# A self-attention block and a residual block on one core: the softmax exponential in two parts, and weight halves kept between image stages that follow each other

## The chip, the core and the metric

The kernel runs on one core of a Trainium2 chip. Its engines work side by side, each on its own stream of instructions: TensorE (PE) multiplies matrices, VectorE (DVE) does elementwise work on two operands, ScalarE (ACT) applies functions to one operand, and GpSimd (POOL) and SyncE (SP) here mostly start transfers. Data lies in DRAM, in the on-chip SBUF (128 partitions), and in PSUM, where TensorE's products are summed. An instruction waits until what it reads has been written and until the buffer it writes is free. An engine's instructions, and a queue's transfer starts, are issued in the order of the program, so one that waits holds those behind it.

The metric is the time of one execution in microseconds (us): 2428.24 us, the median of 3 runs (2428.1 to 2429.0).

## What is computed

Two bottleneck blocks, one after the other, over 16 images of 1024 channels and 32 x 32 pixels, in float32. The first has a local self-attention in its middle, the second a 3x3 convolution. Cut to what matters:

```python
# layer 0: 1x1 to 256 channels, attention over the 3x3 neighbourhood, 1x1 back, residual
h = relu(bn(conv1x1(x, w_conv1)))
q = relu(bn(conv1x1(h, wq)));  k = relu(bn(conv1x1(h, wk)));  v = bn(conv1x1(h, wv))
attn = einsum('bgdhw,bgdkhw->bgkhw', q_heads, unfold3x3(k) + pos)   # 32 heads of 8 channels, 9 taps
attn = softmax(attn, over the 9 taps)
h = relu(bn(einsum('bgdkhw,bgkhw->bgdhw', unfold3x3(v), attn)))
x = relu(bn(conv1x1(h, w_conv3)) + x)
# layer 1: 1x1 to 256 channels, 3x3, 1x1 back, residual
y = relu(bn(conv1x1(x, w1)))
y = relu(bn(conv3x3(y, w2)))
return relu(bn(conv1x1(y, w3)) + x)
```

## The kernel before

The order of TensorE's work is a fixed list of stages. `C` is the first convolution of an image, `Q` its q, k and position products, `V` its v (`P` stands for all three), `F` the fused stage (w_conv3, residual, and the second block's first convolution at once), `W` the 3x3 convolution of four images by the Winograd method, `U` the last convolution of an image. `U10:0123` is a part of the output channels.

```python
"P0 P1 P2 P3 F0 P4 F1 P5 P6 F2 P7 F3 C8 Q8 W0 V8 C9 U0 Q9 V9 U1 U2 U3",
"F4 F5 F6 F7 P10 C11 Q11 W4 V11 C12 U4 Q12 V12 U5 U6 U7",
"F8 F9 P13 F10 F11 C14 Q14 W8 V14 C15 U8 Q15 V15 U9",
"F12 F13 F14 U10:0123 F15 U10:4567 U11:01234 W12 U11:567 U12 U13 U14 U15",
```

VectorE's work is laid beside it by a small model that runs while the program is written: a class `Side` keeps an estimated time of TensorE and one of VectorE and decides after each step of TensorE which pieces of attention or of the Winograd transform are placed next. The values that a piece yields are its estimated us; `EXP` is the time allowed for the exponential, `LATE` how long a transform stands behind attention.

```python
CHUNK, RELAY, EXP, LATE = 3.43, 13.0, 3.0, 30.0
```

The attention of one image is all VectorE but for the exponential, which ScalarE does. `e` holds the 9 taps (256 pixels per partition and tap):

```python
def logits(b):
    ...                                   # 9 taps: products q*k, sums over 8 channels, positions
    mx = apool.tile([P, JPIX], F32, tag="mx", name="mx")
    tree(ALU.max, mx)
    yield 2.7
    nc.vector.tensor_tensor(e, e, mx.unsqueeze(1).to_broadcast([P, KK, JPIX]), ALU.subtract)
    yield 2.6

    yield lambda: nc.scalar.activation(e, e, AF.Exp)
    make_room("qk", b + 1)
    se = apool.tile([P, JPIX], F32, tag="mx", name="se")
    tree(ALU.add, se)
    nc.vector.reciprocal(se, se)
    yield 3.9
    weights_of[b] = e, se

def weighted(b):
    ...
    if b == B - 1:
        fetch_hidden(DEFERRED[0])
    term(0, acc)                          # e[0] * v at tap 0
    yield 2.3
    for k in range(1, KK):
        term(k, t)
        nc.vector.tensor_add(acc, acc, t)
        yield 4.6
    nc.vector.tensor_mul(acc, acc, se ...)
    nc.sync.dma_start(back, acc ...)      # "a" by way of DRAM, read again by the fused stage
    make_room("v", b + 1)
```

q, k and the positions are stored to DRAM from a layout by channels and read again in one by heads and rows; the reading is `relay`, all three tiles at once when the image before has made room:

```python
def relay(what, b):
    if not ((what, b) in written and (what, b) in room_for):
        return
    come[what, b] = max(side.vector, side.tensor) if b else side.tensor
    ...
    for name, tag, shape in shapes:       # q, bnk, pos; or bnv
        t = apool.tile([P] + shape, F32, tag=tag, name=f"{tag}_{b}")
        nc.gpsimd.dma_start(t.rearrange("p d w -> p (d w)"), backs[name])
        moved[name] = ...
```

k and v go out of one buffer, `kp`, by SyncE's queue, the same one that loads the weights and stores the transformed images (`v<-v`):

```python
norm(inside(kp, n), rows(conv(which, n)), name, n, func)    # ScalarE writes kp
nc.sync.dma_start(room[n], AP(block.tensor, ...))           # "bnk<-kp", "bnv<-kp"
```

Weights come in halves of 512 KB into five buffers, four in flight or in use; a new one is loaded when one has had its last use. A fused stage takes four halves, always loaded anew:

```python
if kind == "fused":
    return [("w3", 0), ("u1", 0), ("w3", 1), ("u1", 1)]
...
        before, whose = near.get((name, half), (-9, b))
        if at - before > 3 or name in ("w3", "u1"):
            whose = (b, at)
            queue.append((name, whose, half))
```

In the fused stage the second block's hidden rows end in one buffer, `vh`, from which the Winograd transform of the image is made. Two of the images of the last group store them to DRAM instead, and their transforms are made while F15 runs:

```python
DEFERRED = 13, 14

def fused(b, then):
    side.finish(b)                        # what is left of the image's attention
    if b == B - 1:
        for c in DEFERRED:
            side.first(transform(c, sources[c]) if c in sources else fetched(c), 0.0, 0.0)
    fetch_attended()
    ...
    for o in range(NC + 1):
        if o < NC:
            conv3.products(o)
            ...
        if o:
            reduce_part(o - 1, ps, done.pop(o - 1), "u1")
            if o == NC:
                ...                       # hidden rows into vh
                if b in DEFERRED:
                    kept[b] = dram.tile([P, NW * VROWS * VW], F32, tag=f"h{b}", name="kept")
                    nc.sync.dma_start(kept[b], vh.rearrange("p r w -> p (r w)"))
                else:
                    late = 0.0 if b % NK == NK - 1 else LATE
                    side.first(transform(b, vh), side.tensor + CHUNK + 6.0, side.tensor + late)
```

Of the kernel before, what the change touches and what calls it, by code (L numbers as in the profile page):

```python
# [8 lines left out]
F32 = mybir.dt.float32  # L9
# [4 lines left out]
P = 128  # L14
# [7 lines left out]
KK = 9  # L22
# [7 lines left out]
PW = W + 2  # L30
HALO = (JROWS + 2) * PW
NPOS = 4
G = P // HEAD_DIM
NH = NW * G

# [36 lines left out]
def sa_bottleneck_kernel(ctx: ExitStack, tc: tile.TileContext, x, w1t, wqkvt, w3t, u1t, u2t, u3t, params, out):  # L72
# [275 lines left out]
    def piece(name, half):  # L348
        return name, owner[now[0], name, half], half

    def reduce_part(c, ps, src, name):

        key = piece(name, c * 2 // NC)
        wt = pieces[key]
        for n in range(NW):
            for half in range(2):
                nc.tensor.matmul(  # L357
                    ps[n][:, halves(half)],
                    wt[:, c % (NC // 2), n * P : (n + 1) * P],
                    src[:, halves(half)],  # L360
                    start=(c == 0),
                    stop=(c == NC - 1),
                )
        if c % (NC // 2) == NC // 2 - 1:
            done_with(key)
# [65 lines left out]
    hidden, projected, attended = {}, {}, {}  # L431


    CHUNK, RELAY, EXP, LATE = 3.43, 13.0, 3.0, 30.0

    def by_quarter(name, b, width, per):

# [84 lines left out]

    relaid, written, room_for, come = {}, set(), {("qk", 0), ("v", 0)}, {}

    def relay(what, b):

        if not ((what, b) in written and (what, b) in room_for):
            return  # L530
        come[what, b] = max(side.vector, side.tensor) if b else side.tensor
        moved, backs = projected.setdefault(b, {}), relaid[b]
        if what == "qk":
            shapes = (("q", "qc", [HEAD_DIM, JPIX]), ("bnk", "bnk", [HEAD_DIM, HALO]), ("pos", "pc", [NPOS, JPIX]))
        else:
            shapes = (("bnv", "bnv", [HEAD_DIM, HALO]),)
        for name, tag, shape in shapes:
            t = apool.tile([P] + shape, F32, tag=tag, name=f"{tag}_{b}")
            nc.gpsimd.dma_start(t.rearrange("p d w -> p (d w)"), backs[name])
            moved[name] = t.rearrange("p d (r w) -> p d r w", w=PW) if shape[1] == HALO else t  # L540

    def make_room(what, b):
        room_for.add((what, b))
# [5 lines left out]
    def logits(b):  # L549

        qc, kc = (projected[b][name] for name in ("q", "bnk"))
        e = apool.tile([P, KK, JPIX], F32, tag="e", name=f"e_{b}")
        t = ppool.tile([P, 2, HEAD_DIM, JPIX], F32, tag="t", name="prod")
        for k in range(0, KK, 2):
            of = min(2, KK - k)
            for two in range(of):
                i, j = divmod(k + two, 3)
                nc.vector.tensor_tensor(  # L558
                    by_row(t[:, two]), by_row(qc), kc[:, :, i : i + JROWS, j : j + W], ALU.mult
                )  # L560
# [12 lines left out]
        part = by_tap[:, :, 0:2]  # L573
        nc.vector.tensor_tensor(part, part, pc[:, 2:4].unsqueeze(1).to_broadcast(shape), ALU.add)
        yield 3.5

        def tree(op, to):
            t = zpool.tile([P, 4, JPIX], F32, tag="z", name="tree")
            nc.vector.tensor_tensor(t, e[:, 0:4, :], e[:, 4:8, :], op)
            nc.vector.tensor_tensor(t[:, 0:2, :], t[:, 0:2, :], t[:, 2:4, :], op)  # L580
            nc.vector.tensor_tensor(to, t[:, 0, :], t[:, 1, :], op)
            nc.vector.tensor_tensor(to, to, e[:, 8, :], op)

        mx = apool.tile([P, JPIX], F32, tag="mx", name="mx")
        tree(ALU.max, mx)
        yield 2.7
        nc.vector.tensor_tensor(e, e, mx.unsqueeze(1).to_broadcast([P, KK, JPIX]), ALU.subtract)
        yield 2.6

        yield lambda: nc.scalar.activation(e, e, AF.Exp)  # L590
        make_room("qk", b + 1)
        se = apool.tile([P, JPIX], F32, tag="mx", name="se")
        tree(ALU.add, se)
        nc.vector.reciprocal(se, se)
        yield 3.9
        weights_of[b] = e, se

    weights_of = {}

    def weighted(b):  # L600

        e, se = weights_of.pop(b)
        vc = projected.pop(b)["bnv"]
        both = ppool.tile([P, 2, HEAD_DIM, JPIX], F32, tag="t", name="acc")
        acc, t = both[:, 0], both[:, 1]

        def term(k, dst):
            i, j = divmod(k, 3)
            nc.vector.tensor_tensor(  # L609
                by_row(dst),  # L610
                rows(e[:, k, :]).unsqueeze(1).to_broadcast([P, HEAD_DIM, JROWS, W]),
                vc[:, :, i : i + JROWS, j : j + W],
                ALU.mult,
            )

        if b == B - 1:
            fetch_hidden(DEFERRED[0])
        term(0, acc)
        yield 2.3
        for k in range(1, KK):  # L620
            term(k, t)
            nc.vector.tensor_add(acc, acc, t)  # L622
            yield 4.6
        nc.vector.tensor_mul(acc, acc, se.unsqueeze(1).to_broadcast([P, HEAD_DIM, JPIX]))
        summed[b], back = by_quarter("a", b, JPIX, HEAD_DIM)
        nc.sync.dma_start(back, acc.rearrange("p d w -> p (d w)"))
        make_room("v", b + 1)
        side.ready[b] = side.vector + 2.3 + RELAY
        fetch_attended()
        yield 2.3  # L630
# [210 lines left out]
    class Side:  # L841
# [32 lines left out]
        def step(self):  # L874
            job, self.vector = self.begins()
            if self.exp and not self.held and ("needs" in job or self.exp[0] < self.tensor):
                self.fire()
            cost = next(job["parts"], "end")
            if cost == "end":
                (self.jobs if "needs" in job else self.firsts).remove(job)  # L880
            elif "needs" not in job:
                job["begun"] = True
                cost, rest = cost if isinstance(cost, tuple) else (cost, 0.0)
                self.vector += cost
                job["at"] = self.vector + rest
            elif cost == "v":
                job["needs"] = cost
            elif callable(cost):
                self.exp = self.vector, cost
                if job["b"] == 0:  # L890

                    self.held = True
            else:
                self.vector += cost
# [22 lines left out]
        def passes(self, us, leave=True):  # L917

            self.tensor += us
            if leave:  # L920
                self.run()

# [2 lines left out]
            self.vector = max(self.vector, self.tensor) + us  # L925

        def finish(self, b):
            while any(job["b"] == b for job in self.jobs):
                if self.exp and not self.firsts:
                    self.tensor = max(self.tensor, self.exp[0])  # L930
# [15 lines left out]
    for text in (  # L946
# [5 lines left out]
        for word in text.split():  # L952
            b, _, of = word[1:].partition(":")
            for letter in "CQV" if word[0] == "P" else word[0]:
                kind = {"C": "conv1", "Q": "qk", "V": "v", "F": "fused", "W": "wino", "U": "u3"}[letter]
                stages.append((kind, int(b), [int(o) for o in of] or range(NC)))

    def weights_of_stage(kind, b, of):
        if kind == "conv1":
# [3 lines left out]
        if kind == "v":  # L963
            return [("wv", 0)]
        if kind == "fused":
            return [("w3", 0), ("u1", 0), ("w3", 1), ("u1", 1)]
        if kind == "wino":
            return [(f"U{i}", part) for two in ROWS for part in range(3) for i in two]
        if kind == "u3":
# [5 lines left out]
    for at, (kind, b, of) in enumerate(stages):  # L975
        for name, half in weights_of_stage(kind, b, of):
            before, whose = near.get((name, half), (-9, b))
            if at - before > 3 or name in ("w3", "u1"):
                whose = (b, at)
                queue.append((name, whose, half))  # L980
            owner[at, name, half] = whose
# [31 lines left out]
        return AP(vh.tensor, vh.offset + (n * VROWS + 1) * VW, [vh.ap[0], [9, 4], [VW, H], [1, TR]])  # L1013


    DEFERRED = 13, 14
    kept = {}

    sources = {}
# [9 lines left out]
        yield 0.0, 6.0  # L1029
        yield from transform(b, sources[b])  # L1030

    def fused(b, then):

        side.finish(b)
        if b == B - 1:
# [4 lines left out]
        finish_attended(b)  # L1040
        conv3 = expand("w3", b)
        conv3.src = attended.pop(b)
        following = [(conv3, o) for o in range(2, NC)] + then
        done, ps = {}, None
        for o in range(NC + 1):
            if o < NC:
                conv3.products(o)
                room = stored[b, o] = dram.tile([P, HW], F32, tag=f"r{b}_{o}", name="r")
                done[o] = conv3.result(o, room)
                if o < len(following):  # L1050
                    into, which = following[o]
                    into.seed(which)
                yield CHUNK
            if o:
                ps = ps or two_sums()
                reduce_part(o - 1, ps, done.pop(o - 1), "u1")
                if o == NC:
# [37 lines left out]
    def run(at):  # L1095
# [6 lines left out]
                break  # L1102
        fetch_attended()
        if kind == "fused":
            parts, count = fused(b, then), 2 * NC
        elif kind == "u3":
            parts, count = last_sum(b, of, then), len(of)
        elif kind == "conv1":
# [93 lines left out]
```

## Time and profile before

| | busy, us | share of the span |
|---|---|---|
| TensorE, matmuls | 2387.5 | 98% |
| VectorE | 2081.2 | 86% |
| ScalarE | 917.0 | 38% |
| GpSimd | 467.8 | 19% |
| moved by transfers | 708.38 MB | mean 292 GB/s |

The span of the profiled execution, from its first to its last instruction, is 2426.4 us. A line of the waits says which engine and tile waited, `<-` for whom, how long in total, how many times and the longest. A line of a timeline gives start, duration, engine, line of the program, operation, `out<-in` by the program's names, the shape, the count merged into it, and in brackets the idle time ahead of it with what ended it. `SPq` and `POOL` lines with `DMA` are the starts of transfers, not the transfers. A line of the stretches has, behind the busy time and the count of each engine, three columns: the clock that TensorE was granted (1.00 is full), the share of the transfer engines, and GB/s.

### The profile page before, as it was taken

Reading aid. Unit: us, or ns where it says so; the run is one execution under the profiler, and the core shown is the slowest. Engines: PE = TensorE matmul, PEld = TensorE weight load, DVE = VectorE, ACT = ScalarE, POOL = GpSimd, SP = SyncE. Lnnn points to the kernel's source line nnn. Section 1 sums busy time; section 2 is a strip of 40 time slices with the busy share of each in tenths; the row PEclk is TensorE's granted clock in tenths of the full one; section 3 lists DMA queues with packets and bytes.
Section 4 is the critical chain, followed back from the end, with each engine's and each line's share of the span. In section 5 each row is a group of like instructions: output and inputs, shape, how many; then the busy total and the mean of one; then the engine's idle time right before and its main releaser. Section 6 shows DMA issues by size and latency. Waiting matters only on the chain.

```text
span 2426.4 us, 18497 instructions
## 1 busy us (share of the span) xinstructions
PE 2387.5 (98%) x6144; PEld 1150.3 (47%) x6144; DVE 2081.2 (86%) x1632; ACT 917.0 (38%) x873; POOL 467.8 (19%) x854
## 2 busy tenths in 40 slices
PE   8999999999999999999999999999999999999999
PEld 3443434444466444444466444444466444434844
DVE  4899988999999989999989999998989999965700
ACT  3323242233222474433122574324222553344265
POOL 2111111111111232111111232112111221112132
PEclk9999999999999999999999999999999999999999
DMA  9969686887797899797788998689788897888887
GB/s 359 360 208 313 228 274 227 258 300 236 288 310 254 333 355 352 261 307 250 246 296 277 318 375 337 238 287 320 244 307 305 310 350 250 279 310 292 320 295 251
DMA packets 305822, 708.38 MB, mean 292 GB/s; under 512 B 20544, under 2 KB 174144, under 8 KB 297024
## 3 DMA queue, kind: packets, MB, share of 16 engines
q0 software_dynamic: 119024, 471.40, 53.3%
q1 hardware_dynamic: 185264, 231.30, 29.7%
q10 hardware_dynamic: 1440, 4.51, 0.5%
q8 instruction: 49, 0.80, 0.1%
q14 instruction: 45, 0.37, 0.0%
HBM read 432.10 MB, written 275.03 MB: 291 GB/s over the span
## 4 chain that ended last, share of the span: by engine, by line
PE 85%; DMA 5%; DVE 5%; issue 2%; ACT 1%; POOL 1%; SPq 0%; ACTq 0%; POOLq 0%; DVEq 0%
PE ps L357 34%; PE ps L389 30%; PE ps L452 11%; PE ps L744 8%; DMA U<-uw 2%; DVE acc L609 2%; DVE acc L622 2%; DMA bnk<-kp 1%; PE ps L490 1%; DMA a<-acc 1%; DMA a<-a 1%; ACT h L1004 1%; DMA uw<-u 0%; POOL out_dram L417 0%; DMA v<-v 0%
## 5 line engine op out<-in xcount | busy, mean ns | idle before, releaser
L389 PE MATMUL ps<-a,w 128*128 128x512 f32 x1024 | 461.7, 596 | 5.1 <-ACT a L648 4.8
L357 PE MATMUL ps<-result,u 128*128 128x512 f32 x1024 | 460.1, 594 | 6.6 <-ACT result L416 6.6
L357 PE MATMUL ps<-x,w 128*128 128x512 f32 x1024 | 445.1, 595 | 6.2 <-DMA x<-in_x_dram 6.2
L389 PE MATMUL ps<-y,u 128*128 128x512 f32 x1024 | 443.2, 594 | 4.2 <-ACT ps L380 4.2
L609 DVE TENSOR_TENSOR acc<-e,bnv 128x2048 f32<-128x2048 f32 x144 | 327.6, 2284 | 3.6
L558 DVE TENSOR_TENSOR prod<-qc,bnk 128x2048 f32<-128x2048 f32 x144 | 324.1, 2287 | 1.7
L389 PEld LDWEIGHTS ps<-a,w 128*128 128x128 f32 x1024 | 195.2, 191 | 253.5 <-issue 243.0
L357 PEld LDWEIGHTS ps<-result,u 128*128 128x128 f32 x1024 | 194.9, 191 | 254.0 <-issue 238.1
L357 PEld LDWEIGHTS ps<-x,w 128*128 128x128 f32 x1024 | 195.6, 191 | 252.5 <-issue 252.0
L389 PEld LDWEIGHTS ps<-y,u 128*128 128x128 f32 x1024 | 194.9, 191 | 250.6 <-issue 241.0
L416 ACT ACTIVATE result<-ps,par 128x1024 f32<-128x1024 f32 x128 | 142.5, 1113 | 442.6 <-PE ps L389 371.6
L622 DVE TENSOR_TENSOR acc<-acc 128x2048 f32<-128x2048 f32 x128 | 293.4, 2292 | 4.4
L452 PE MATMUL ps<-h,wqk 128*128 128x512 f32 x512 | 225.8, 595 | 5.7 <-ACT h L1004 5.7
L417 POOL DMA_DIRECT2D r<-result x128 | 69.0, 539 | 637.3 <-ACT result L416 622.4
L416 ACT ACTIVATE result<-ps,bn_sh 128x1024 f32<-128x1024 f32 x127 | 141.2, 1112 | 133.0 <-PE ps L389 122.4
L563 DVE TENSOR_TENSOR prod<-prod 128x2048 f32<-128x2048 f32 (+1 forms) x80 | 166.2, 2077 | 2.4
L452 PEld LDWEIGHTS ps<-h,wqk 128*128 128x128 f32 x512 | 96.2, 190 | 132.7 <-issue 110.0
L1004 ACT ACTIVATE h<-ps,par 128x1024 f32<-128x1024 f32 x32 | 38.4, 1204 | 283.2 <-PE ps L357 283.0
L380 ACT ACTIVATE ps<-r 128x1024 f32<-128x1024 f32 x128 | 130.4, 1020 | 29.3 <-DMA r<-r 21.8
L464 ACT ACTIVATE kp<-ps,par 128x1024 f32<-128x1024 f32 x64 | 77.4, 1210 | 168.5 <-PE ps L452 125.7
L380 ACT ACTIVATE ps<-s 128x1024 f32<-128x1024 f32 x128 | 131.2, 1025 | 2.5
L339 POOL DMA_DIRECT2D x<-in_x_dram x120 | 64.0, 534 | 298.2 <-PE ps L357 231.2
(317 smaller groups left out, 2294.5 us busy)
## 6 DMA issues: line engine op xcount, KB each, us to landing
s<-in_x_dram POOLq DMA_DIRECT2D x128, 512.0 KB, 7.1
r<-result POOLq DMA_DIRECT2D x128, 512.0 KB, 4.8
r<-r POOLq DMA_DIRECT2D x128, 512.0 KB, 6.5
out_dram<-result POOLq DMA_DIRECT2D x127, 512.0 KB, 6.3
x<-in_x_dram POOLq DMA_DIRECT2D x120, 512.0 KB, 5.0
v<-v SPq DMA_DIRECT2D x96, 408.0 KB, 4.4
U<-uw SPq DMA_DIRECT2D x72, 512.0 KB, 5.5
bnk<-kp SPq DMA_DIRECT2D x32, 680.0 KB, 7.8
```

Source lines behind the costliest of these rows:

```text
L357: nc.tensor.matmul(ps[n][:, halves(half)], wt[:, c % (NC // 2), n * P : (n + 1) * P], src[:, halves(half)], start=(c == 0), stop=(c == NC ...
L380: nc.scalar.activation(ps, loaded.pop((self.kind, self.b, o)), AF.Identity)
L389: nc.tensor.matmul(self.ahead[o][:, halves(half)], pieces[key][:, n, o % (NC // 2) * P :][:, :P], self.src[:, n, halves(half)], start=Fals ...
L416: nc.scalar.activation(to_, ps, RELU, bias=self.shift(o), scale=1.0)
L417: nc.gpsimd.dma_start(to, t)
L452: nc.tensor.matmul(ps[:, halves(half)], pieces[key][:, m, at : at + P], h[:, m, halves(half)], start=(m == 0), stop=(m == NW - 1),)
L464: nc.scalar.activation(dst, src, func, bias=col(f"L0_conv_{name}_b", n), scale=col(f"L0_conv_{name}_s", n),)
L558: nc.vector.tensor_tensor(by_row(t[:, two]), by_row(qc), kc[:, :, i : i + JROWS, j : j + W], ALU.mult)
L563: nc.vector.tensor_add(u[:, :, 0:4], u[:, :, 0:4], u[:, :, 4:8])
L609: nc.vector.tensor_tensor(by_row(dst), rows(e[:, k, :]).unsqueeze(1).to_broadcast([P, HEAD_DIM, JROWS, W]), vc[:, :, i : i + JROWS, j : j ...
L622: nc.vector.tensor_add(acc, acc, t)
L744: nc.tensor.matmul(acc[i][:, at, :, n, :], pieces[key][:, m, at, n * P : (n + 1) * P], v[:, at, :, m * (TILES + TR) :][:, :, :TILES], star ...
```

## The change

It has four parts.

- The subtraction of the maximum and the exponential are made in two parts, of 4 and of 5 taps. The sum over the taps and its reciprocal move from ahead of the weighted terms to behind the first four of them, so that VectorE has terms of the first part to work on while ScalarE does the second. The model's figures follow (`EXP` 2.0).
- A fused stage that directly follows another one takes over the halves of the weights that lie there. Its output channels run in the reverse order of halves, so that it begins with those that the one ahead ended with.
- Of the last group only image 13's hidden rows are sent through DRAM; image 14's transform is made from `vh`, as for other images.
- From image 2 on, the three tiles of a relay are fetched one after the other, `GAP` (5 us of TensorE's model time) apart.

```diff
+FIRST = 4
...
-    def reduce_part(c, ps, src, name):
+    def reduce_part(c, ps, src, name, first=0, last=NC - 1):
...
-                    start=(c == 0),
-                    stop=(c == NC - 1),
+                    start=(c == first),
+                    stop=(c == last),
...
-    CHUNK, RELAY, EXP, LATE = 3.43, 13.0, 3.0, 30.0
+    GAP = 5.0
+    CHUNK, RELAY, EXP, LATE = 3.43, 13.0, 2.0, 30.0
...
+    moves = []
+    def more_moves(now):
+        while moves and moves[0][0] <= now:
+            moves.pop(0)[1]()
...
-        come[what, b] = max(side.vector, side.tensor) if b else side.tensor
...
-        for name, tag, shape in shapes:
+        def move(name, tag, shape):
             t = apool.tile([P] + shape, F32, tag=tag, name=f"{tag}_{b}")
             nc.gpsimd.dma_start(t.rearrange("p d w -> p (d w)"), backs[name])
             moved[name] = ...
+            if len(moved) in (3, 4):
+                come[what, b] = max(side.vector, side.tensor) if b else side.tensor
+        for i, shape in enumerate(shapes):
+            if b < 2 or i == 0:
+                move(*shape)
+            else:
+                moves.append((side.tensor + GAP * i, lambda shape=shape: move(*shape)))
...
-        nc.vector.tensor_tensor(e, e, mx.unsqueeze(1).to_broadcast([P, KK, JPIX]), ALU.subtract)
-        yield 2.6
-        yield lambda: nc.scalar.activation(e, e, AF.Exp)
+        parts = [e[:, :FIRST], e[:, FIRST:]]
+        for part in parts:
+            nc.vector.tensor_tensor(
+                part, part, mx.unsqueeze(1).to_broadcast([P, part.shape[1], JPIX]), ALU.subtract
+            )
+        yield 2.7
+        def exps():
+            for part in parts:
+                nc.scalar.activation(part, part, AF.Exp)
+        yield exps
         make_room("qk", b + 1)
-        se = apool.tile([P, JPIX], F32, tag="mx", name="se")
-        tree(ALU.add, se)
-        nc.vector.reciprocal(se, se)
-        yield 3.9
-        weights_of[b] = e, se
+        weights_of[b] = e, tree
...
-        if b == B - 1:
+        if b == B - 1 and DEFERRED and DEFERRED[0] in kept:
             fetch_hidden(DEFERRED[0])
         term(0, acc)
         yield 2.3
         for k in range(1, KK):
+            if k == FIRST:
+                se = apool.tile([P, JPIX], F32, tag="mx", name="se")
+                tree(ALU.add, se)
+                nc.vector.reciprocal(se, se)
+                yield 4.6
             term(k, t)
...
+                if kind == "fused" and stages and stages[-1][0] == "fused" and stages[-1][2][0] == 0:
+                    order = order[NC // 2 :] + order[: NC // 2]
...
-            return [("w3", 0), ("u1", 0), ("w3", 1), ("u1", 1)]
+            return [(name, half) for half in (of[0] * 2 // NC, of[-1] * 2 // NC) for name in ("w3", "u1")]
...
-            if at - before > 3 or name in ("w3", "u1"):
+            if at - before > (3 if name[1:] != "3" and name != "u1" or name == "u3" else 1):
...
-    DEFERRED = 13, 14
+    DEFERRED = (13,)
...
-    def fused(b, then):
+    def fused(b, of, then):
...
-        for o in range(NC + 1):
-            if o < NC:
+        for at in range(NC + 1):
+            if at < NC:
+                o = of[at]
```

More of the change, by code (lines that the diff above doesn't have):

```diff
@@ L586, in logits @@
         yield 2.7
-        nc.vector.tensor_tensor(e, e, mx.unsqueeze(1).to_broadcast([P, KK, JPIX]), ALU.subtract)
-        yield 2.6
-        yield lambda: nc.scalar.activation(e, e, AF.Exp)
-        make_room("qk", b + 1)
-        se = apool.tile([P, JPIX], F32, tag="mx", name="se")
-        tree(ALU.add, se)
-        nc.vector.reciprocal(se, se)
-        yield 3.9
-        weights_of[b] = e, se
+        parts = [e[:, :FIRST], e[:, FIRST:]]
[8 more added lines that the diff above has]
+        yield exps
+        make_room("qk", b + 1)
+        weights_of[b] = e, tree
     weights_of = {}
     def weighted(b):
-        e, se = weights_of.pop(b)
+        e, tree = weights_of.pop(b)
         vc = projected.pop(b)["bnv"]
@@ L888, in step @@
             elif callable(cost):
-                self.exp = self.vector, cost
+                self.exp = self.vector - 0.0, cost
                 if job["b"] == 0:
@@ L919, in passes @@
             self.tensor += us
+            more_moves(self.tensor)
             if leave:
@@ L927, in finish @@
         def finish(self, b):
+            more_moves(1e6)
             while any(job["b"] == b for job in self.jobs):
@@ L955, in sa_bottleneck_kernel @@
                 kind = {"C": "conv1", "Q": "qk", "V": "v", "F": "fused", "W": "wino", "U": "u3"}[letter]
-                stages.append((kind, int(b), [int(o) for o in of] or range(NC)))
+                order = [int(o) for o in of] or list(range(NC))
+                if kind == "fused" and stages and stages[-1][0] == "fused" and stages[-1][2][0] == 0:
+                    order = order[NC // 2 :] + order[: NC // 2]
+                stages.append((kind, int(b), order))
     def weights_of_stage(kind, b, of):
@@ L1042, in fused @@
         conv3.src = attended.pop(b)
-        following = [(conv3, o) for o in range(2, NC)] + then
+        following = [(conv3, o) for o in of[2:]] + then
         done, ps = {}, None
-        for o in range(NC + 1):
-            if o < NC:
+        for at in range(NC + 1):
+            if at < NC:
+                o = of[at]
                 conv3.products(o)
@@ L1049, in fused @@
                 done[o] = conv3.result(o, room)
-                if o < len(following):
-                    into, which = following[o]
+                if at < len(following):
+                    into, which = following[at]
                     into.seed(which)
                 yield CHUNK
-            if o:
+            if at:
                 ps = ps or two_sums()
-                reduce_part(o - 1, ps, done.pop(o - 1), "u1")
-                if o == NC:
+                reduce_part(of[at - 1], ps, done.pop(of[at - 1]), "u1", of[0], of[-1])
+                if at == NC:
                     side.finish_firsts()
@@ L1104, in run @@
         if kind == "fused":
-            parts, count = fused(b, then), 2 * NC
+            parts, count = fused(b, of, then), 2 * NC
         elif kind == "u3":
```

## The prediction

> **What bounds the kernel now.** I read the page's first part, then the waits of TensorE, then the timelines of the stretches where those waits fall.
>
> ```profile
> PE 2387.5 (98%) x6144; PEld 1150.3 (47%) x6144; DVE 2081.2 (86%) x1632; ACT 917.0 (38%) x873; POOL 467.8 (19%) x854
> ```
>
> TensorE is busy for 98% of the span, VectorE for 86%. So the order of matmuls is the bound and everything else matters only where TensorE waits. A busy share says little of the pitch, so I made a floor of it from the timeline: 8 matmuls of 512 columns start every 3.43 us, 0.429 us each; the 288 matmuls of an undisturbed 3x3 stage take 62.3 us, 0.216 us each; the 8 position products 1.87 us. That gives 4864 x 0.429 + 1152 x 0.216 + 128 x 0.233 = 2367 us. With 6.2 us ahead of the first matmul and 4.8 us after the last it makes 2378 us, of a span of 2426.4. **About 49 us can be lost to waits at all**, and nothing in the change removes a matmul.
>
> ```profile
> engine line waited for: us in total, times, longest us
> PE ps L357 <- ACT result L416: 6.6, 2, 5.2
> PE ps L357 <- DMA x<-in_x_dram: 6.2, 1, 6.2
> PE ps L452 <- ACT h L1004: 5.7, 13, 0.4
> PE ps L389 <- ACT a L648: 4.8, 2, 4.3
> PE ps L389 <- ACT ps L380: 4.5, 3, 3.2
> PE ps L744 <- DMA U<-uw: 4.2, 4, 1.7
> ```
>
> These are few and single waits. By stage, as the excess over the pitch: image 0's fused stage F0 3.7 us (from 207), F1 7.3 (324 to 341), the first 3x3 stage W0 2.2, the output sum U1 5.1 (at 851), F15 8.3 (2145), the last 3x3 stage W12 3.0, the sums after it 1.5. The other part is fixed: 13 waits for h at 0.8 us each, and the start (3 us of slow matmuls, 2 us for q).
>
> A long wait costs twice. Here are the stretches around F1's wait and around F15's; PEclk is the last column but two:
>
> ```profile
> 336.00:342.00 6.00, 5.87 (x10) 2.60 (x11) 5.93 (x6) 2.95 (x4) 2.15 (x4) 0.68 1.12 290
> 2144.00:2156.00 12.00, 10.60 (x17) 4.23 (x18) 10.72 (x12) 4.16 (x5) 1.07 (x2) 0.72 0.73 268
> ```
>
> The clock was 0.68 and 0.72 there, 1.00 before and after. F15's wait of 4.30 us is followed by 16 matmuls in 10.82 us in place of 6.87: 8.3 us in all.
>
> **VectorE decides when F15 may begin.** VectorE runs image after image with hardly a gap; its one repeated gap is the exponential:
>
> ```profile
> DVE tree L579 <- ACT e L590: 44.9, 16, 8.0
> ```
> ```profile
> 2080.77 2.11 ACT L590 ACTIVATE e<-e 128x2304 f32<-128x2304 f32 x1
> ```
> ```profile
> 2082.92 1.23 DVE L579 TENSOR_TENSOR tree<-e 128x1024 f32<-128x1024 f32 x1 [2.60 <-ACT e L590]
> 2126.85 2.29 DVE L624 TENSOR_TENSOR acc<-acc,se 128x2048 f32<-128x2048 f32 x1
> 2136.67 1.50 DVE L673 SCALAR_TENSOR_TENSOR form<-hidden 128x612 f32<-128x612 f32 x2 [7.52 <-DMA a<-acc]
> ```
>
> In all 16 images VectorE stands at least 2.1 us while ScalarE does e; 44.9 us in sum. The last image's acc is done at 2129.1, its way through DRAM (a<-acc, then a<-a) ends at 2143.6, and TensorE, which came to F15 at 2140.6, waits until 2144.9.
>
> **What the Trainium skill says.** (1) "TensorE: Matmul & The Clock Gate", section "What's actually happening": after an idle window of about 3.4 us the clock is gated to half and needs a busy window to come back. The two clocks above agree, and so does the 3.0 us lost after the start. (2) "Perfetto Trace Analysis", section "Optimizing Scalar/DVE Operations": where Scalar or Vector isn't saturated but causes bubbles, breaking up instructions may let work finish sooner, at an overhead per instruction. The trace agrees on the overhead: 256 elements take 0.425 us, 512 take 0.69, 1024 take 1.22, so some 0.16 us are fixed. (3) "DMA: Bandwidth & Descriptors", section "Anatomy of one DMA": a semaphore wait happens on the issuing sequencer, ahead of dispatch. So a store whose data isn't ready holds what is behind it in the queue. F1 shows it:
>
> ```profile
> 318.64 1.40 SPq L709 DMA_DIRECT2D v<-v  x2
> 320.09 1.75 SPq L129 DMA_DIRECT2D w<-ws  x1
> 321.93 1.53 SPq L476 DMA_DIRECT2D bnk<-kp  x1
> ```
> ```profile
> 333.87 1.21 ACT L464 ACTIVATE kp<-ps,par 128x1024 f32<-128x1024 f32 x1 [10.58 <-DMA bnk<-kp]
> ```
>
> kp was written at 316.4, yet its store went out at 321.9, behind v<-v, which waited for VectorE until 318.6. ScalarE then stood 10.6 us for the buffer kp, results behind it came late, and TensorE waited 5.2 us.
>
> **The change, part by part.**
>
> *Exponential in two parts (4 and 5 taps), tree and reciprocal moved behind four terms.* Removed: VectorE's wait for e. The second subtraction (5 x 256 = 1280 elements, 1.48 us by the rows above) runs while ScalarE does the first part (1024 elements; 2.11 x 4/9 plus a fixed part, some 1.05 us). So the first four terms can begin at once, and the second part (some 1.3 us) is long done when the tree needs it, 16 us later. Added: the split subtraction, 1.22 + 1.48 - 2.56 = 0.14 us. Over 16 images: 44.9 removed, some 5 left where ScalarE is itself late, 2 added: **VectorE runs some 35 us ahead of before by the last image, if nothing else holds it.** I count on 15 to 30, as the 3x3 stages tie VectorE to TensorE. F15's attention would need to be only 4.3 us earlier, so that wait goes: **-8.3 us**. By F1 two exponentials are past (4.4 and 2.2 us waited); v<-v is then ready near 313 and bnk<-kp is not held: I take 5 of the 7.3: **-5**. F0's wait begins with a<-a, which follows image 0's attention, some 4 us earlier: **-2.5**. At 834 the store of kp took 15.4 us beside a<-acc and the loads for F4; with a<-acc ten us earlier this may lose its crowd: 5.1 at even odds, **-2.5**.
>
> *Weights kept in directly following fused stages.* By the stage list these are F4 to F7, F8 F9, F10 F11, F12 to F14; every follower may take all four halves over, as the rule reloads only if the last use is more than one stage back. That is 3 + 1 + 1 + 2 = 7 stages x 4 loads = 28 loads of 512 KB, 14.7 of 708 MB, 2%. TensorE never waited for w or u, nor anywhere in these stages but 0.6 us: **0** of itself. The reversed order changes which half is freed first in the last stage of a run, not how many loads are in flight.
>
> *Only image 13's hidden rows go by DRAM.* Removed: a store and a load of 1.3 MB, and VectorE's 12.6 us wait for hidden at 2173. Image 14's transform now reads vh after F14. But VectorE's next work, image 15's transform, waits for F15's end at 2205 anyway (6.9 us idle there), so it is off the path. And image 13's rows may be fetched later than now, as its transform stands second. Then image 15's transform may begin late relative to F15. W12 has little to spare: its first V loads go out at 2227.5, take some 5 us, and W12 begins at 2234.7, so 2 us of delay are free and more would be waited for: **+2**.
>
> *Relay in three steps 5 us apart.* It begins at an exponential and is needed by the next image's logits some 45 us later, so 10 us more cost nothing; the queues are smoother. **0**.
>
> Sum: -8.3 - 5 - 2.5 - 2.5 + 2 = -16. Every shift of VectorE also reshuffles the transfers, with the DMA engines at 60 to 100% in all slices, so I allow 4 us for new waits of the sort that U1 and W0 have now. 2428.2 - 16 + 4 = **2416 us**.
>
> **Rivals.** *The waits move on*: the single waits are chance meetings of transfers, and an earlier VectorE meets others; one new wait over 3.4 us costs 5 to 8 us with the slow clock. For it: F1 and U1 both came from a store that met a crowd. Against: the long middle, 930 to 2120, has only 0.6 us of it in spite of all its variety. Result: about 2424 to 2430. *The tail gives it back*: without the wait F15 ends 8 us earlier, but image 13's late fetch and image 15's transform then hold W12 for as long. For it: VectorE ended the second transform only 7 us before the third. Against: VectorE could be idle from some 2105, and image 14's transform starts as soon as vh is there. Result: about 2421. *The kept halves block SyncE's queue*: a weight load waits for a half that is still in use and stops the stores behind it. For it: stores already wait there. Against: halves of u3 are held over the whole of W12 now while 36 other pieces pass through the same five buffers, so free ones are found out of order. Result: 2440 and more, at a few per cent.
>
> **Range and chances.** The floor with the fixed losses is some 2393 us, which caps the gain at 1.4%; a loss over 2% (48 us) would need six new long waits or a blocked queue. I say **2416 us**, 2406 to 2428 in 8 of 10; the upper end is no gain, the lower has nearly every avoidable wait gone. Chances: faster by over 2% 0.01, within 2% 0.97, slower by over 2% 0.02.
>
> **What would show it.** Right: VectorE's wait for e under 10 us in sum; no wait for a at F15 and a clock of 1.00 there; acc of image 15 done before 2115; F1's wait under 2 us; 36 loads of w and u in place of 64; W12 not later than 31 us after F15. Wrong: TensorE's waits still near 34 us in sum at other places, W12 waiting for V, or SyncE's weight loads waiting long in F5 to F14.

## The result, and the profile after

The changed kernel takes 2415.1 us (median of 4 runs, 2414.2 to 2416.3), beside 2428.2 of the kernel before: 0.9947 of it, 95% interval 0.9929 to 0.9964. On another occasion it took 2414.9 us beside 2424.8 (9 and 36 runs): 0.9961 (0.9946 to 0.9975). The predicted 2416 us is met; the gain is 13.1 us on the first occasion and 9.9 on the second, where 12.2 was predicted. By which waits it is met is another matter.

The waits of TensorE in the changed kernel, longest in total first (us in total, times, longest):

```profile
PE ps L390 <- ACT a L675: 8.9, 2, 5.0
PE ps L358 <- DMA x<-in_x_dram: 6.6, 1, 6.6
PE ps L454 <- ACT h L1037: 5.7, 13, 0.4
...
PE ps L358 <- ACT result L417: 1.3, 1, 1.3
PE ps L390 <- ACT ps L381: 1.0, 1, 1.0
```

The wait for U (4.2 us before) is not in the list any more, those for results and for ps have shrunk from 6.6 and 4.5 us, and the wait for a, which the prediction saw gone, has grown from 4.8 to 8.9. VectorE still waits for the exponential:

```profile
DVE acc L631 <- ACT e L613: 32.4, 8, 10.1
```

It was 44.9 us in 16 places, 12 of them of 2.1 to 2.2 us and the longest of 8.0; it is 32.4 in 8 places, one of 10.1 and one of 8.7. So half of the images are free of it, and a few wait longer than before.

The table turns this into losses by stage. A loss is the time from a stage's first matmul to the next stage's first, less its matmuls at their pitch (0.429, 0.216 and 0.233 us, as in the prediction), so it holds the wait at the stage's end and the slow matmuls after a wait. F15 is F15 and the sums directly ahead of it. Each row is one profiled execution; those from the fourth on are the experiments below.

| loss in us | F0 | F1 | W0 | U1 | F15 | W12 | all stages |
|---|---|---|---|---|---|---|---|
| before | 2.2 | 7.3 | 2.3 | 5.1 | 8.4 | 3.1 | 49.0 |
| changed | 0.0 | 1.8 | 0.2 | 0.0 | 12.0 | 0.3 | 35.0 |
| changed, again | 2.4 | 0.0 | 0.2 | 0.0 | 10.1 | 2.8 | 33.9 |
| weights alone | 0.1 | 8.1 | 8.7 | 6.8 | 7.3 | 3.5 | 56.1 |
| hidden rows alone | 3.9 | 1.7 | 2.2 | 4.8 | 8.1 | 2.8 | 44.6 |
| relay alone | 1.5 | 7.0 | 2.5 | 4.8 | 8.5 | 2.0 | 46.6 |
| all but the split | 1.7 | 6.2 | 2.2 | 2.2 | 9.0 | 2.8 | 44.1 |
| split alone | 0.0 | 7.1 | 0.2 | 0.0 | 13.7 | 0.6 | 40.5 |
| work moved ahead of F15 | 0.3 | 5.7 | 0.2 | 0.0 | 2.9 | 5.0 | 39.6 |
| before, no reciprocal | 1.2 | 4.1 | 0.3 | 1.9 | 8.5 | 2.8 | 36.6 |
| last exponential ahead | 2.1 | 0.6 | 0.2 | 0.0 | 4.5 | 4.3 | 30.4 |
| all attention ahead | 0.0 | 2.3 | 2.3 | 0.0 | 4.6 | 6.1 | 52.1 |
| u3 freed besides | 0.0 | 0.7 | 0.2 | 0.9 | 2.9 | 3.4 | 28.2 |
| relus ahead besides | 1.2 | 4.1 | 0.2 | 0.0 | 0.2 | 3.1 | 27.8 |

One profile is not proof of one wait. "Weights alone" and "hidden rows alone" have the same instructions as the kernel before up to U1, yet F1 lost 8.1 and 1.7 us in them and 7.3 in the other, and W0 8.7, 2.2 and 2.3. In the changed kernel again F1 lost 0.0 us, where I had expected 2 or 7. The kernel before took anything from 2419 to 2439 us in 50 runs, and the profile of "weights alone" is of its slowest run, 2435.9 us. What can be trusted are columns that sort themselves by what is in the kernel: W0 and U1 do, F15 does, F1 does in part, F0 and W12 do not.

### The profile page after: what moved, and what is told of

It reads as the page before. It is cut to its first block, busy times and chain, and to the rows that moved or that the text cites. A ratio compares the mean times of both kernels' runs of the same rounds, so it can differ in the third digit from the quotient of the medians.

```text
span 2412.5 us, 18460 instructions
## 1 busy us (share of the span) xinstructions
PE 2381.2 (99%) x6144; PEld 1149.3 (48%) x6144; DVE 2080.5 (86%) x1648; ACT 919.6 (38%) x889; POOL 467.9 (19%) x854
## 3 DMA queue, kind: packets, MB, share of 16 engines
q1 hardware_dynamic: 175568, 213.97, 27.8%
## 4 chain that ended last, share of the span: by engine, by line
PE 86%; DVE 5%; issue 4%; DMA 3%; ACT 1%; POOL 1%; POOLq 0%; SPq 0%; ACTq 0%; DVEq 0%
PE ps L358 34%; PE ps L390 30%; PE ps L454 11%; PE ps L771 10%; DVE acc L631 2%; DVE acc L649 1%; PE ps L492 1%; DMA a<-a 1%; POOL out_dram L418 1%; DMA a<-acc 1%; POOL r L340 1%; ACT h L1037 1%; DMA uw<-u 0%; DMA s<-in_x_dram 0%; DVE y L797 0%
## 5 line engine op out<-in xcount | busy, mean ns | idle before, releaser
L631 DVE TENSOR_TENSOR acc<-e,bnv 128x2048 f32<-128x2048 f32 x144 | 327.6, 2284 | 35.4 <-ACT e L613 32.4
```

The source lines that it names most:

```text
L631: nc.vector.tensor_tensor(by_row(dst), rows(e[:, k, :]).unsqueeze(1).to_broadcast([P, HEAD_DIM, JROWS, W]), vc[:, :, i : i + JROWS, j : j ...
```

## The experiments

Theory: the split lets VectorE run ahead of TensorE, and that lead removes waits that come from late stores. Rival: the traffic became thinner (28 weight loads, 2.6 MB of hidden rows and the bunched relays less). Each ratio is to the kernel before, run beside it.

**The four parts, each alone on the kernel before.** Their edits are those of the diff above, sorted by part.

The split (`FIRST`, both `parts` loops, the sum behind the fourth term, `EXP` and the yields):

> The kernel before with the exponential in two parts alone. My theory: the split lets VectorE run ahead, and that takes the waits of F0 (-2), F1 (-5), W0 (-2) and U1 (-5) away, so this part alone makes nearly all of the gain: 2414 to 2419 us. Rival (transfers): the gain comes from the 28 weight loads left out, which thin the traffic; then this kernel stays near 2426 us and F1, W0 and U1 still wait. Both expect F15 to wait 4 us or more still.

Measured: 2418.6 us, 0.9965 (0.9954 to 0.9976). W0 and U1 are gone, F15 waits more, 13.7 us. The theory holds for the whole and for W0 and U1; F1 still lost 7.1 us.

The weights (`reduce_part`'s `first` and `last`, the order of halves, the rule of reloading):

> The kernel before with the kept weight halves alone. My theory: 2427 to 2429 us, no wait of TensorE changes but by chance, as all of its waits lie outside the followers F5 to F7, F9, F11, F13, F14. Rival (transfers): 2416 to 2422 us, with less waiting for kp, a and U.

Measured: 2427.9 us, 1.0005 (0.9993 to 1.0017). Nothing, as the theory has it.

Image 14's hidden rows kept on the chip (with the guard on `kept`):

```diff
-    DEFERRED = 13, 14
+    DEFERRED = (13,)
```

> The kernel before with image 13 alone sent through DRAM. My theory: the wait of the last 3x3 stage for U (3 us) goes, as 2.6 MB less run beside the last group, and the rest stays: 2424 to 2427 us. Rival: nothing of the gain is from here, 2428 us, and the 3 us at the last 3x3 stage went with the earlier VectorE.

Measured: 2423.7 us beside 2425.2, 0.9995 (0.9984 to 1.0005). W12 still lost 2.8 us. My expectation for this part fell.

The relay in three steps (`moves`, `GAP`):

> The kernel before with the relay in three steps alone. My theory: 2427 to 2429 us, as no wait of TensorE began at a relay. Rival (transfers): the crowds at W0 and U1 thin out, 2420 to 2424 us.

Measured: 2424.4 us beside 2425.2, 0.9996 (0.9987 to 1.0005). W0 and U1 lost what they lost before.

**All but the split.** The changed kernel with the exponential, the sum and the reciprocal as they were:

> The changed kernel with the exponential in one piece as before, the other three parts in. My theory: the gain goes, 0.998 to 1.000 of the kernel before, with the waits of W0, U1 and F0 back (2, 5, 2 to 4 us) and VectorE waiting over 40 us for e. Rival (the parts help one another, the three others giving what the split alone does not): 0.995 to 0.998.

Measured: 2424.7 us beside 2424.8, 1.0005 (0.9997 to 1.0014); VectorE waited 40.7 us for e. The gain is gone. W0 lost 2.2 us again; U1 lost 2.2, not the 5 that I expected. With the split alone at 0.9965 and the whole at 0.9947 and 0.9961, the split is nearly all of it, and thinner traffic is none that can be seen.

**Is it the lead, or the changed order?** The kernel before without the reciprocal: `se` is left as the sum, so the output is not divided by it but multiplied. Nothing else is changed, the exponential stays in one piece.

```diff
         tree(ALU.add, se)
-        nc.vector.reciprocal(se, se)
```

> The kernel before, with its exponential in one piece, but without the reciprocal of the softmax sum (the output is then weighted by the sum in place of divided by it). Every other instruction and its order is the same. It gives VectorE 1.75 us per image, 28 us by the end. My theory (all that the split does is to let VectorE run ahead): W0 loses 0 to 1 us in place of 2 and U1 0 to 1 in place of 5, F15 loses 4 to 12, and the whole is 0.995 to 0.998 of the kernel before. Rival (the split works by the changed order of issue: the exponential's place, the sum behind the terms, the model's figures): W0 and U1 wait as before, 0.999 to 1.001.

Measured: 2416.2 us, 0.9961 (0.9948 to 0.9973): the same gain as the split, without any part of the change. W0 lost 0.3 us, U1 1.9 (5.1 before, 0 to 1 expected). VectorE still waited for e after each subtraction, 51.2 us in all:

```profile
DVE tree L579 <- ACT e L590: 51.2, 16, 6.9
```

So 28 us less work for VectorE gain as much as the split, with the exponential in one piece and in its old place. A lead alone is enough for a gain of this size; that it comes at the same waits is shown for W0, and for U1 in part: the two make 5.2 of the 12.4 us less that its profile lost.

U1 shows how a lead gets to TensorE. SyncE's queue and ScalarE, kernel before and changed kernel:

```profile
830.65 0.34 SPq L626 DMA_DIRECT2D a<-acc  x1
831.08 0.69 SPq L129 DMA_DIRECT2D w<-ws  x1
833.86 0.37 SPq L476 DMA_DIRECT2D bnk<-kp  x1
```
```profile
849.37 1.21 ACT L464 ACTIVATE kp<-ps,par 128x1024 f32<-128x1024 f32 x1 [9.12 <-DMA bnk<-kp]
```
```profile
818.08 0.34 SPq L653 DMA_DIRECT2D a<-acc  x1
818.51 0.38 SPq L130 DMA_DIRECT2D w<-ws  x1
825.09 0.37 SPq L478 DMA_DIRECT2D bnk<-kp  x1
```
```profile
834.03 1.21 ACT L466 ACTIVATE kp<-ps,par 128x1024 f32<-128x1024 f32 x1 [2.56 <-DMA bnk<-kp]
```

a<-acc, 1 MB, leaves when VectorE has finished an image. Before, it left 3.2 us ahead of the store of kp, and that store took 15.5 us (833.86 to 849.37); changed, it left 7.0 us ahead, and the store took 8.9. ScalarE waited 2.6 us for the buffer in place of 9.1, and the seed behind it came in time (a seed is ScalarE's write of the residual into PSUM, `ps<-s` or `ps<-r`, onto which TensorE adds the products of a sum).

The other profiles agree. In all five without a lead a<-acc leaves 3.2 us ahead and the store of kp takes 14.2 to 15.8 us. Without the reciprocal it leaves 4.9 us ahead (13.8 us), and in the eight with the split 7.0 us or more (7.0 to 12.9 us): there a<-acc has landed before the store begins. W0's wait of 1.7 us was for a load of U, issued as W0 began: it took 15.8 us in the kernel before and 8.2 in the changed kernel.

**Where the lead is lost.** In the changed kernel image 15's exponential stands, on ScalarE, behind a seed; on VectorE, the terms wait for it:

```profile
2065.35 1.02 ACT L381 ACTIVATE ps<-s 128x1024 f32<-128x1024 f32 x1
2066.29 2.20 ACT L613 ACTIVATE e<-e 128x1024 f32<-128x1024 f32 x2
```
```profile
2056.04 2.63 DVE L606 TENSOR_TENSOR e<-e,mx 128x1024 f32<-128x1024 f32 x2
2067.37 4.49 DVE L631 TENSOR_TENSOR acc<-e,bnv 128x2048 f32<-128x2048 f32 x2 [8.70 <-ACT e L613]
```

Both subtractions were done at 2058.7. ScalarE was idle in between for 1.4 and 2.1 us at a time, but the program has two results and two seeds ahead of the exponential, and these wait for TensorE. To move it ahead of them, the last image's attention is issued further ahead; VectorE's own order stays.

```diff
-                if self.exp and not self.held and self.exp[0] < self.tensor + 4.0:
+                ahead = 11.0 if self.jobs and self.jobs[0]["b"] == B - 1 else 4.0
+                if self.exp and not self.held and self.exp[0] < self.tensor + ahead:
                     self.fire()
-                if self.begins()[1] >= self.tensor + 4.0:
+                if self.begins()[1] >= self.tensor + ahead:
```

> The changed kernel, with the last image's attention issued up to 11 us ahead in place of 4, so that its exponential stands two results earlier in ScalarE's order; VectorE's order is the same. My theory: F15 waits because VectorE's lead is lost where that exponential stands behind results that wait for TensorE (8.7 us of waiting); then VectorE waits about 1 us for e, image 15's acc is done some 7 us earlier, F15 loses 1 to 5 us in place of 12, and the whole is 6 to 10 us below the changed kernel. Rival (the way through DRAM is what is slow, 21 us from acc to the last a, and the crowd decides): acc is earlier, but F15 still loses 8 us or more, and the whole gains 3 us at most.

Measured: 2409.2 us beside 2414.9 of the changed kernel on the same occasion; 0.9943 (0.9928 to 0.9959). VectorE and TensorE:

```profile
2058.14 4.49 DVE L631 TENSOR_TENSOR acc<-e,bnv 128x2048 f32<-128x2048 f32 x2 [1.03 <-ACT e L613]
```
```profile
2126.86 9.07 PE L390 MATMUL ps<-a,w 128*128 128x512 f32 x16 [2.33 <-ACT a L675]
```

The wait for e is 1.0 us, acc leaves at 2104.3 in place of 2113.5, and F15 loses 4.5 us in place of 12.0 and 10.1. The way through DRAM was shorter too, 15.5 us from acc's store to the last a (2104.3 to 2119.8) in place of 21.3. It did not decide: 21.3 us would have ended at 2125.6 (an estimate from these numbers), just when ScalarE came to a. So the theory holds in each of these; the whole gains 5.7 us by the medians, and the intervals of the two ratios overlap.

**Work moved in front of F15 instead.**

```diff
-"F12 F13 F14 U10:0123 F15 U10:4567 U11:01234 W12 U11:567 U12 U13 U14 U15",
+"F12 F13 F14 U10:0123 U11:01 F15 U10:4567 U11:2345 W12 U11:67 U12 U13 U14 U15",
```

> The changed kernel with two of the sums of image 11 (6.9 us of matmuls) moved ahead of F15, and one more kept behind it. Both theories agree that F15's wait comes from image 15's attention being late against TensorE: F15 loses 0 to 5 us in place of 12. The stretch between F15 and the last 3x3 stage is one sum (3.4 us) shorter: if the forms of image 15 have no slack, that stage waits up to 3.4 us more. The whole: 4 to 10 us below the changed kernel.

Measured: 2418.9 us, 0.9976 (0.9967 to 0.9985), slower than the changed kernel by the medians (2414.9). F15 and the sums ahead of it lost 2.9 us in place of 12.0, so most of the wait did go. But W12 lost 5.0 (0.3 and 2.8 in the changed kernel), the sums between F15 and W12 1.8, and the two sums left behind W12 4.6 (1.2 before), as the seed for the next image waited for VectorE's end of W12, which three sums had covered. The gain was given back at the next two seams. My 4 to 10 us were wrong: I had counted one shortened stretch, not both.

**All attention issued ahead.** The `ahead` above as 11.0 for every image:

> The changed kernel with the attention of every image issued up to 11 us ahead in place of 4, not the last one's alone. If VectorE's waiting for e (31 us in eight places) is worth taking away everywhere: waiting for e under 8 us and a time at or below that of the last image alone, 0.992 to 0.995 of the kernel before. Rival: an exponential that is issued before VectorE has its operand holds ScalarE's results behind it, and the early stores hold SyncE's queue: new waits of TensorE for results and kp, 0.996 to 1.002.

Measured: 2430.0 us, 1.0017 (1.0009 to 1.0024). Slower, and VectorE's waiting for e grew where I expected under 8 us:

```profile
DVE acc L631 <- ACT e L613: 51.6, 9, 16.5
```

The 16.5 us are image 0's: its exponential came on ScalarE behind two writes of h, which had waited 24.5 us for TensorE. The largest new wait of TensorE came in a way that I had not named. GpSimd's queue, and TensorE in the stage of image 3's first convolution:

```profile
171.02 0.56 POOL L340 DMA_DIRECT2D x<-in_x_dram  x1 [8.18 <-PE ps L358]
189.31 0.54 POOL L546 DMA_DIRECT2D bnv<-bnv  x1 [17.73 <-DVE acc L631]
189.85 1.05 POOL L340 DMA_DIRECT2D x<-in_x_dram  x2
```
```profile
196.94 9.95 PE L358 MATMUL ps<-x,w 128*128 128x512 f32 x16 [9.05 <-DMA x<-in_x_dram]
```

The relay of v was put into the queue before VectorE had freed its tile, stood there for 17.7 us, and the loads of x stood behind it. TensorE waited 9.1 us, and 16 matmuls then took 9.95 us in place of 7.0. An engine that is issued ahead must not carry with it the transfers that wait for it.

**The last 3x3 stage.** With the last exponential ahead, the halves of u3 are given up before W12 and loaded again behind it:

```diff
-            if at - before > (3 if name[1:] != "3" and name != "u1" or name == "u3" else 1):
+            across = name == "u3" and any(stage[0] == "wino" for stage in stages[max(before, 0) : at])
+            if across or at - before > (3 if name[1:] != "3" and name != "u1" or name == "u3" else 1):
```

> The kernel with the last image's exponential ahead, and besides the two halves of the last convolution's weights given up ahead of the last 3x3 stage and loaded again behind it, so that three of its own weights can be on their way in place of two. My theory: that stage waits for U because only two loads are under way; it then loses under 1.5 us in place of 3 to 4, and the whole is 1 to 4 us below the kernel with the exponential ahead, 0.991 to 0.995 of the kernel before. Rival (the crowd of stores around it makes it wait): it still loses 3 us or more.

Measured: 2409.2 us, 0.9934 (0.9915 to 0.9953). W12 still lost 3.4 us. The loads did leave earlier: the fourth of U at 2210.5 in place of 2218.4, ahead of W12's start at 2213.8. But the third, for which W12 waits, still took 13.8 us (14.4 without this edit). So the theory of too few loads on their way fell; whether the crowd is the cause was not tried by itself and stays open. The whole cannot be told from the kernel with the exponential ahead.

**The last 2.3 us at F15.** In six of the profiles F15 had a wait of 2.3 us for a. In the kernel with the exponential ahead ScalarE did the two relus on a from 2125.6 to 2127.9 with no idle time ahead of them, directly behind image 10's last result. One more edit puts them ahead of that result:

```diff
         hooks["conv1", 2, 0] = clear_hidden
+        hooks["u3", 10, 2] = lambda: finish_attended(B - 1)
```

> The kernel with the last image's exponential ahead and u3 freed, and besides the two relus on image 15's a, which begin F15, issued on ScalarE one result earlier. My theory: the 2.3 us that TensorE still waits at F15 are these two relus of 1.2 us behind the last result of image 10; a is there some 4 us earlier, so the wait goes: F15 loses under 0.7 us, and the whole is 2 to 3 us below the last kernel, 0.991 to 0.994 of the kernel before. Rival (a itself lands only then): ScalarE stands waiting for a, holds results, and F15 still loses 2 us or more.

Measured: 2407.0 us, 0.9913 (0.9895 to 0.9930), the lowest of all, though its interval overlaps that of the kernel without this edit. ScalarE and TensorE:

```profile
2125.90 2.37 ACT L675 ACTIVATE a<-a,par 128x1024 f32<-128x1024 f32 x2
2128.17 1.01 ACT L381 ACTIVATE ps<-s 128x1024 f32<-128x1024 f32 x1
2129.11 1.10 ACT L417 ACTIVATE result<-ps,bn_sh 128x1024 f32<-128x1024 f32 x1
```
```profile
2113.61 13.90 PE L390 MATMUL ps<-y,u 128*128 128x512 f32 x32
2127.35 7.25 PE L390 MATMUL ps<-a,w 128*128 128x512 f32 x16
```

F15 follows without a wait and loses 0.2 us. The order of ScalarE alone took away the last part of F15's loss, as expected.

## Why the prediction was right, and where it was not

The total was right to 1 us on the first occasion; the terms were not, so that closeness is luck: errors cancelled. By the prediction's own steps:

- **TensorE is the bound, and about 49 us can be lost**: right (with the pitches as rounded there the sum of the matmuls is 2365 us, not 2367). The loss fell from 49.0 to 35.0 us, the busy time of the matmuls hardly moved (2387.5 to 2381.2), and the time followed the loss: 13.9 us in the profiles.
- **The split, -8.3 at F15**: wrong in sign. F15 lost 12.0 and 10.1 us in place of 8.4. VectorE did run ahead: image 15's acc was done 15.7 us earlier (2113.5 for 2129.1), within "15 to 30" and before the 2115 that was named as a sign. The step that failed is "F15's attention would need to be only 4.3 us earlier, so that wait goes". It sets the attention against the time at which TensorE used to come. But TensorE came earlier too, as the prediction's own -5, -2.5 and -2.5 ahead of F15 demand. Before and changed, TensorE at the end of F14 (the first product behind it) and VectorE at acc (the line of before is in the prediction):

```profile
2126.68 13.90 PE L389 MATMUL ps<-y,u 128*128 128x512 f32 x32
```
```profile
2112.20 13.90 PE L390 MATMUL ps<-y,u 128*128 128x512 f32 x32
2111.18 2.29 DVE L651 TENSOR_TENSOR acc<-acc,se 128x2048 f32<-128x2048 f32 x1
```

  TensorE was 14.5 us earlier, so the attention gained 1.2 us on it and no more. It had gained 7.1 at the subtractions (done at 2058.7 in place of 2080.3, 21.6 us earlier); then VectorE waited 8.7 us for e in place of 2.6, which took 6.1 back. I took the time of an exponential as the cost to remove and left out that its place in ScalarE's order is fixed by the model, beside results that wait for TensorE: "some 5 left where ScalarE is itself late" was 32.4. That this place kept F15's wait from going was shown by moving it: F15 then lost 4.5. That the loss even grew has another source: a's way through DRAM took longer. Before, ScalarE came to the second half of a at 2145.7; then ScalarE and TensorE in the changed kernel:

```profile
2145.65 1.24 ACT L648 ACTIVATE a<-a,par 128x1024 f32<-128x1024 f32 x1 [0.83 <-DMA a<-a]
```
```profile
2128.65 1.24 ACT L675 ACTIVATE a<-a,par 128x1024 f32<-128x1024 f32 x1 [1.41 <-DMA a<-a]
2134.78 1.24 ACT L675 ACTIVATE a<-a,par 128x1024 f32<-128x1024 f32 x1 [4.89 <-DMA a<-a]
```
```profile
2129.95 1.13 PE L390 MATMUL ps<-a,w 128*128 128x512 f32 x2 [3.85 <-ACT a L675]
2136.07 8.85 PE L390 MATMUL ps<-a,w 128*128 128x512 f32 x14 [5.00 <-ACT a L675]
```

  From acc's store to the second half of a it is 21.3 us (2113.5 to 2134.8) where it was 16.5 (2129.2 to 2145.7): 4.8 us more, against the 1.2 gained. Why the way was longer was not tried and stays open. So F15 waits twice, 3.9 and 5.0 us, and behind the second wait 14 matmuls take 8.85 us, where 6.2 would do.
- **U1, -2.5 "at even odds"**: right in mechanism, and worth nearly all of the 5.1 in every kernel that has the split (0.9 left in one). **W0** was not counted and gave 2.1, in all but one of them (all attention ahead, where TensorE waited 2.1 us at W0 for ScalarE, which had itself waited 6.8 us for VectorE). These two are what the lead bought most surely; U1 without the split but with the other three parts lost 2.2, so part of its 5.1 can vary without a lead.
- **F1, -5, and F0, -2.5**: F1 lost 5.5 us less, but not shown to be by the change. v<-v left at 315.7, not near 313, and kp's store still stood behind it: 2.6 us from kp's end (315.2) to the store's start (317.8), where it was 5.5. "Hidden rows alone", with no lead, shows the same 2.6. Over the profiles this delay was 2.6 to 6.7 us without a lead for VectorE (5.0 or more in four of five) and 1.6 to 3.5 with one, while the store itself took 9.6 to 13.0 us in either case. So a lead shortens the delay, as the prediction has it, but does not remove it, and F1 lost 1.7 to 8.1 us without a lead and 0 to 7.1 with one. The -2.5 at F0 isn't shown: its 3.7 us held 1.4 lost just ahead of F0; the two together are 2.0 and 2.9 in the two profiles of the changed kernel.
- **Weights 0, relay 0**: right, 1.0005 and 0.9996. That the kept halves don't block SyncE's queue was right as far as TensorE shows it: F4 to F14 lost under 0.6 us each. The sign of a long wait did come, one weight load stood 70.2 us in the queue until it left in F9 (20.1 before). But the next start behind it, v<-v, left only 15.5 us after it.
- **Hidden rows, +2 at W12**: wrong. W12 lost 0.3 and 2.8 us in the two profiles of the changed kernel, 3.1 before; no delay. VectorE stood idle for 20 us ahead of image 15's transform, so image 13's late rows cost nothing.
- **New waits, +4**: the sum needed it, but no wait appeared at a new place; what came nearest in size is the growth of F15's loss, by 1.7 and 3.6 us. So the -16 + 4 = -12 came out as -14 in that profile: -7.2 from U1 and W0, -10.5 from F1, F0 and W12, which chance has a hand in, and +3.6 from F15 in place of -8.3.

Of the rivals, the one that "the waits move on" came nearest in kind, though not in its 2424 to 2430 us: the growth at F15 is its sort. The tail that gives everything back fitted the version with work moved ahead of F15, not the change.

## What to carry to other kernels

A wait of a helper engine that is repeated in every round can be worth removing even if the main engine does not wait for it there: here the lead it gave took single late stores off TensorE's path. But a lead can be lost at the next operation that hands over to an engine with a fixed order, so check what stands ahead of that operation there before counting the lead to the end. And count a lead against the time at which the main engine will come after the change, not against the time at which it came before. And before giving a single wait a cause, look at a second execution of the same program.

## What the runs showed of the hardware that was not expected

- The same program's time ranged over 20 us (2419 to 2439 in 50 runs), and the loss of a single stage over 6 us (F1 lost 7.3, 8.1 and 1.7 us with the same instructions up to there).
- The Trainium skill ("TensorE: Matmul & The Clock Gate", "What's actually happening") puts the clock's fall at an idle window of about 3.4 us. The slow matmuls behind F15's wait of 5.0 us agree (14 in 8.85 us in place of 6.2). Shorter waits were followed by a lower clock here too, but not always. Behind a wait of 2.95 us (the changed kernel, again) 2 matmuls took 2.07 us in place of 1.0. A single wait of 2.33 us was followed by 16 matmuls in 7.41 us at a clock of 1.00 in two kernels (work moved ahead, u3 freed) and in 9.07 and 9.10 us at a lowered clock in two others (last exponential ahead, all attention ahead); 7.0 is full pitch. One stretch of each sort, first with the last exponential ahead, then with the work moved ahead (the clock is the last column but two):

```profile
2126.00:2137.00 11.00, 10.13 (x19) 4.28 (x20) 3.23 (x4) 4.95 (x5) 1.58 (x3) 0.84 0.84 256
```
```profile
2134.00:2146.00 12.00, 9.66 (x23) 3.94 (x22) 3.75 (x5) 6.99 (x7) 1.78 (x5) 1.00 0.79 282
```
